# Layer 1 of a convolution and state-space kernel: transposes of delta x and sums of squares moved on TensorE, the first y sum of each group one step later, 432 instead of 416 tokens of the C products on VectorE

## The chip, the core and the metric

The kernel runs on one core of a Trainium2 chip. The core has TensorE (PE, matrix products and transposes), VectorE (DVE), ScalarE (ACT), GpSimd (POOL), SyncE (SP, which here issues the DMAs) and 16 DMA engines. The metric is the device time of one execution in microseconds; all data are float32.

## What is computed

Layer 0 is a block of convolutions on x of shape (32, 96, 56, 56). Layer 1, where the change lies, takes its result as 32 sequences of 3136 tokens with 96 channels and applies two blocks of this kind, then a 1x1 convolution with a batch normalisation:

```python
h = (seq - mu) * rsqrt(var + EPS) * ln_g + ln_b
xs, z = jnp.split(h @ in_w, 2, axis=-1)              # 192 channels each
xc = silu(sum(conv_w[:, k] * xp[:, k:k + L, :] for k in range(4)) + conv_b)
dbl = xc @ xproj_w                                   # dt, B (16), C (16)
delta = softplus(dt @ dt_w + dt_b)
dA = exp(delta[..., None] * A)
dBx = delta[..., None] * Bm[:, :, None, :] * xc[..., None]
hstates = associative_scan(comb, (dA, dBx), axis=1)[1]   # h = dA * h + dBx along the tokens
y = einsum('blds,bls->bld', hstates, Cm) + Dp * xc
seq = seq + (y * silu(z)) @ out_w
```

There are 192 x 16 = 3072 states per sequence, and each needs its own recurrence along the tokens.

## The kernel before

**Units and scans.** Each sequence is cut into four chunks of 784 tokens (`LC`). A unit is one chunk in one of the two blocks, so there are 256 units, in an order that alternates the blocks. In a unit the 3072 states are 24 tiles of 128 partitions (4 states by 32 channels). Each tile is one scan of 784 tokens on VectorE (L1052), one per step `at` of the main loop (L1134 on). `place` gives for step t of a unit a group k (of 64 channels, eight steps), j (which four states, two steps) and p (which 32 channels).

**Around one scan.** A scan needs da, an exponential of ScalarE (`decay`, L1004), and the input term. For j = 0 TensorE makes that term in PSUM (`fill`, L1018, 64 small matmuls of transposed u = delta x with diagonals of B). For j = 1 to 3 GpSimd makes it for two tiles at once (`inject`, bx, L1041). The states are then multiplied by C, two tiles at once: the first `LP` tokens on VectorE (`product`, L1060, with a copy cp of C that ScalarE puts into PSUM, `bring`, L1029), the rest on GpSimd (`rest`, L1068). TensorE sums the products over the states into y (`reduce`, L1099, 8 matmuls for two tiles). ScalarE starts each y with Dp x (`seed`, L1086), and VectorE multiplies the finished y by the gate (`gated`, L1110). There is one PSUM bank for y, so a seed waits for the gating of the group before. The fills are the scans 0, 1, 8, 9, 16 and 17 of a unit. A fill and a da tile of the other scans share two PSUM slots in turn, so fill t starts when scan t - 2 has ended.

**The order of the work** is written out by hand. In each step the loop issues, in this order: the steps of other units due below .05 of the step, the seed of tile at - 4 (`LAG` = 4), decays, the C copy, bursts, the scan, gating, VectorE's product, a save of the last state, GpSimd's product, the fill of the next step, the due steps from .05 to .08, the y sum of tile at - 4, and the other due steps. Each engine runs its own instructions in that order.

**The next unit is prepared meanwhile.** `prepare` gives each preparatory step a due time in steps; modulo 24 it tells at which scan of the running units it is issued. Those in question here: `center` (two matmuls per half, cen, L702) and `square` (ScalarE, sx, L707) at steps 12 to 14; `variance` (var, 14 matmuls with a single column, L712) at 14.06; `root` (L719 to 721) at 16.1, three small VectorE steps (`newton`) at 17.7; `turn_u` (ut, four transposes of u each, L848) at steps 19.5, 5.6 and 6.3 for the three groups, and `keep_u` (two ScalarE copies from PSUM, L854 and L855) half a step later. u itself is made by GpSimd (`input_u`, L864) at steps 9.5, 10.5 and 11.5. The results of such steps pass through two PSUM banks, taken in turn (`bank`). The convolution (xs, L773), the projections (bc L798, dt L810, z L789) and a burst of Silu or Softplus on ScalarE (L677, with table loads on either side) fall between. `finish` makes the output of a unit (o, L905 and L909) a unit later.

## Time and profile before

| | |
|---|---|
| median of 3 runs | 18177.14 us (18168.33 to 18189.24) |
| profiled execution, its own time | 18204.1 us |
| span in its trace | 18202.3 us |
| layer 1, first scan to end of the last | 3055.5 to 17903.5 us |
| granted TensorE clock, mean | 0.912 |
| busy VectorE, TensorE, ScalarE, GpSimd in 8000 to 12000 us | 3776.5, 3471.1, 3379.7, 3799.7 us |
| DMA engines' share, moved, in the same 4000 us | 0.71, 184 GB/s |
| mean C product on VectorE, on GpSimd | 998 ns, 1760 ns |
| mean C copy on ScalarE | 513 ns |

A line of a timeline has the start in us, the time taken, the engine, the line of the kernel, the operation, its tiles (out<-in) with their size, how many were merged, and in brackets the engine's idle time before it with what ended that. A line of the waits has the waiting engine and tile, what it waited for, the total in us, how often, and the longest. A line of the windows has the stretch, its length, the busy time of PE, PE's weight loads, DVE, ACT and POOL (with the number of instructions), then the granted TensorE clock, the DMA engines' share and GB/s.

### The profile page before, as it was taken

How to read it: one execution, taken by the hardware profiler on the slowest of the kernel's cores; microseconds unless marked ns; L12 is line 12 of the kernel's file. 1: busy time of each engine (PE TensorE's matmuls, PEld its weight loads, DVE VectorE, ACT ScalarE, POOL GpSimd, SP SyncE). 2: the span in 40 equal slices, each digit the busy share in tenths (PEclk: the TensorE clock that was granted, in tenths of full speed). 3: DMA queues.
4: the chain of work that ended last, by engine and by line, in shares of the span. 5: the costliest groups of instructions: out<-in, count | busy, mean ns of one | idle time of the engine just before them, and what ended most of it. 6: DMA issues, size and time to landing. Idle time of an engine off the chain costs nothing.

```text
span 18202.3 us, 515600 instructions
## 1 busy us (share of the span) xinstructions
PE 15733.6 (86%) x212542; PEld 8423.4 (46%) x212542; DVE 16751.8 (92%) x12755; ACT 14204.1 (78%) x26476; POOL 14151.6 (78%) x6254
## 2 busy tenths in 40 slices
PE   9999998888888888888888888888888888888882
PEld 4444444444444444444444444444444444444441
DVE  9999996999999999999999999999999999999993
ACT  5555555888888888888888888888888888888884
POOL 0000002999999999999999999999999999999993
PEclk9999998999999999999999999999999999999996
DMA  1111113777777777777777777777777777777768
GB/s 35 29 29 29 29 29 88 182 183 183 182 185 186 184 183 183 183 183 186 184 183 182 183 182 186 184 184 183 183 183 184 186 183 182 184 182 182 186 182 220
DMA packets 1723533, 2893.14 MB, mean 159 GB/s; under 512 B 712886, under 2 KB 950670, under 8 KB 1714790
## 3 DMA queue, kind: packets, MB, share of 16 engines
q1 hardware_dynamic: 1712534, 2821.54, 59.6%
q0 software_dynamic: 6656, 38.54, 1.0%
q8 instruction: 1668, 27.33, 0.6%
q14 instruction: 691, 5.66, 0.1%
q10 hardware_dynamic: 1984, 0.07, 0.0%
HBM read 2402.42 MB, written 455.82 MB: 157 GB/s over the span
## 4 chain that ended last, share of the span: by engine, by line
PE 22%; ACT 16%; issue 12%; DMA 11%; DVE 9%; SPq 7%; POOL 5%; ACTq 0%; POOLq 0%; DVEq 0%
PE bp L1018 9%; DVE hh L1052 5%; ACT da L1004 5%; ACT bx L1004 4%; SPq L982 4%; DVE hc L1060 3%; DMA bdiag<-bt 3%; DMA deltab<-deltad 3%; PE y L1099 3%; SPq L969 3%; POOL hc L1068 2%; POOL bx L1041 2%; PE bc L798 2%; PE o L909 2%; DMA C<-bcd 2%
## 5 line engine op out<-in xcount | busy, mean ns | idle before, releaser
L1041 POOL TENSOR_TENSOR bx<-ub,B 128x1568 f32<-128x1568 f32 x2304 | 8160.7, 3542 | 16.2 <-DMA B<-bcd 16.2
L1052 DVE TENSOR_TENSOR_SCAN hh<-da,state,bx 128x784 f32<-128x784 f32 x3456 | 6257.5, 1835 | 53.1 <-ACT da L1004 50.2
L1068 POOL TENSOR_TENSOR hc<-hh,C 128x736 f32<-128x736 f32 x3072 | 5407.9, 1760 | 747.9 <-DVE hh L1052 476.0
L1004 ACT ACTIVATE da<-deltab,acol 128x784 f32<-128x784 f32 x4608 | 4253.4, 923 | 1192.4 <-DVE hh L1052 1184.8
L1099 PE MATMUL y<-hc,rel 128*32 128x392 f32 x24576 | 2888.8, 544 | 551.0 <-ACT y L1086 547.4
L1018 PEld LDWEIGHTS bp<-diag,ut 91*32 91x32 f32 (+1 forms) x98304 | 2873.9, 131 | 931.9 <-DVE hh L1052 544.1
L1018 PE MATMUL bp<-diag,ut 91*32 91x91 f32 (+1 forms) x98304 | 3192.1, 293 | 116.6 <-DVE hh L1052 100.7
L1060 DVE TENSOR_TENSOR hc<-hh,cp 128x832 f32<-128x832 f32 x3072 | 3065.6, 998 | 0.1
L1052 DVE TENSOR_TENSOR_SCAN hh<-bx,state,bp 128x784 f32<-128x784 f32 x1152 | 2116.7, 1837 | 491.3 <-PE bp L1018 488.6
masks.py:197 POOL MEMSET eye<- 128x128 f32 x2 | 0.4, 204 | 2923.3 <-ACT x L427 2923.0
L773 PE MATMUL xs<-xn,wx 97*64 97x392 f32 x12288 | 2250.3, 508 | 0.5 <-ACT xc L784 0.4
L1052 DVE TENSOR_TENSOR_SCAN hh<-da,bx 128x784 f32<-128x784 f32 x1152 | 2017.9, 1774 | 29.6 <-ACT da L1004 28.1
L340 DVE SCALAR_TENSOR_TENSOR h<-hpad,hp,h 128x1568 f32<-128x1568 f32 x1024 | 1895.3, 1851 | 33.2
L1029 ACT COPY cp<-C 128x416 f32<-128x416 f32 x3072 | 1576.4, 513 | 95.6 <-DVE hc L1060 93.3
L1004 ACT ACTIVATE bx<-deltab,acol 128x784 f32<-128x784 f32 x1536 | 1467.8, 956 | 0.0
L773 PEld LDWEIGHTS xs<-xn,wx 97*64 97x64 f32 x12288 | 816.5, 137 | 1357.4 <-issue 1264.4
L1099 PEld LDWEIGHTS y<-hc,rel 128*32 128x32 f32 x24576 | 623.9, 118 | 1523.9 <-ACT y L1086 1044.7
L307 PE MATMUL dw<-hpad,diag 32*32 32x392 f32 x36864 | 1124.8, 525 | 0.6 <-issue 0.4
L1052 DVE TENSOR_TENSOR_SCAN hh<-bx,bp 128x784 f32<-128x784 f32 x384 | 683.0, 1779 | 244.2 <-PE bp L1018 228.3
L245 PE MATMUL c<-x,w 96*128 96x392 f32 x2048 | 785.3, 526 | 118.2 <-ACT hpad L252 96.2
L848 PE MATMUL ut<-eye,us 128*91 128x128 f32 (+1 forms) x3072 | 582.3, 320 | 340.7 <-ACT xc L784 340.3
L307 PEld LDWEIGHTS dw<-hpad,diag 32*32 32x32 f32 x36864 | 680.8, 106 | 375.4 <-issue 132.0
(195 smaller groups left out, 20083.7 us busy)
## 6 DMA issues: line engine op xcount, KB each, us to landing
ub<-ud SPq DMA_DIRECT2D x3072, 196.0 KB
deltab<-deltad SPq DMA_DIRECT2D x3072, 196.0 KB
C<-bcd SPq DMA_DIRECT2D x4096, 98.0 KB
diag<-bdiag SPq DMA_DIRECT2D x1024, 294.8 KB
B<-bcd SPq DMA_DIRECT2D x3072, 98.0 KB
deltad<-dl SPq DMA_DIRECT2D x512, 294.0 KB
ud<-us SPq DMA_DIRECT2D x1536, 98.0 KB
x<-in_x_dram SPq DMA_DIRECT2D x32, 1176.0 KB
```

The lines of the kernel that those rows point to most:

```text
L245: pe.matmul(ps[:p, k, :HB], w1[:, ct * 128 : ct * 128 + p], xs[b][:, c0 : c0 + HB], start=True, stop=True)
L307: pe.matmul(ps[r][to : to + 32, :HB], diag[src, n, t, :], hb[src, r0 : r0 + RB, dx : dx + W], start=t == 0, stop=t == 8, skip_group_check= ...
L340: v.scalar_tensor_tensor(acc, src, tap, acc, ALU.mult, ALU.add)
L773: pe.matmul(d["xs", k][h * 64 : h * 64 + 64, :HB], wx[:, i, o, k * 64 : k * 64 + 64], xn[:, o + h * HB : o + h * HB + HB], start=o == 0, s ...
L1004: s.activation(das[at], d["delta", k][:, p, :], AF.Exp, scale=acol[:, j, i, 2 * k + p : 2 * k + p + 1])
L1018: pe.matmul(ps[sg * DB : sg * DB + DB, o : o + z], d["ut", k][:z, b, h, p * DB : p * DB + DB], dg[:z, sg // 2, h, x : x + z, sg % 2], star ...
L1029: s.copy(cps[at], data[n]["C", j][:, :LP])
L1041: g.tensor_mul(bx, data[n]["u", k], beside(data[n]["B", j]))
L1052: v.tensor_tensor_scan(hhs[at - p][:, p, :], das.pop(at), bxs.pop(at), state[i][:, t : t + 1] if c % NQ else 0.0, ALU.mult, ALU.add,)
L1060: v.tensor_mul(hcs[at - 1][:, :, :LP], hhs[at - 1][:, :, :LP], beside(cps.pop(at)))
L1068: g.tensor_mul(hcs[at - 1][:, :, LP:], hhs[at - 1][:, :, LP:], beside(data[n]["C", j][:, LP:]))
L1099: pe.matmul(yps[k][r0 : r0 + DB, :HB], rel, hc[:, p, h * HB : h * HB + HB], start=False, stop=j == SG - 1, skip_group_check=True,)
```

## The change

Four edits, all in layer 1.

- `LP` goes from 416 to 432: VectorE multiplies 432 of 784 tokens by C, GpSimd 352, and the copy of C grows with it.
- The transposes of u (`turn_u`, `keep_u`) go to steps 13.06 and 14.06 (copies at 14.005 and 15.01) of the unit before for the first two groups, and to 19.5 (copy at 20.1) for the third.
- `variance` goes from step 14.06 to 15.06, which is after the fill of scan 16 and before the y sum in the same step; the second `center` goes behind the first transpose of its step.
- All seeds go one step later (`LAG` + 1), and so does the y sum of the tiles with j = 0; the other y sums stay.

```diff
-LP = 416
+LP = 432
...
-                steps += [((-11.9, -10.94)[h], lambda h=h: center(h)), ((-10.98, -9.99)[h], lambda h=h: square(h))]
-            steps += [(-9.94, variance), (-7.9, root), *[(t, lambda m=m: newton(m)) for m, t in enumerate((-6.3, -6.2, -6.1))]]
+                steps += [((-11.9, -10.93)[h], lambda h=h: center(h)), ((-10.98, -9.99)[h], lambda h=h: square(h))]
+            steps += [(-8.94, variance), (-7.9, root), *[(t, lambda m=m: newton(m)) for m, t in enumerate((-6.3, -6.2, -6.1))]]
...
-                steps += [((43.5, 53.6, 54.3)[k], lambda k=k: turn_u(k)), ((44.1, 54.2, 55.01)[k], lambda k=k: keep_u(k))]
+                steps += [((37.06, 38.06, 43.5)[k], lambda k=k: turn_u(k)), ((38.005, 39.01, 44.1)[k], lambda k=k: keep_u(k))]
...
-                if 0 <= at - LAG < total:
-                    seed(at - LAG)
+                if 0 <= at - LAG - 1 < total:
+                    seed(at - LAG - 1)
...
-                if 0 <= at - LAG < total:
-                    reduce(at - LAG)
+                for t in (at - LAG - 1, at - LAG):
+                    if 0 <= t < total and by_pe(t) == (t == at - LAG - 1):
+                        reduce(t)
```

## The prediction, as put on record

> **What bounds the kernel now.** I read the page's busy table first, then the sums of waits in a steady stretch (4,000 to 16,000 us), then the timelines of VectorE and TensorE through one unit, then the granted clock in the windows that stood out.

> ```profile
> PE 15733.6 (86%) x212542; PEld 8423.4 (46%) x212542; DVE 16751.8 (92%) x12755; ACT 14204.1 (78%) x26476; POOL 14151.6 (78%) x6254
> ```

> Layer 1 runs from 3,056 to 17,903 us: 256 units of 24 scans, 58.02 us each (mean of units 20 to 239; every "unit time" below is that mean, counted from the unit's scan 0). VectorE needs 24 scans, 12 C products, 3 gatings and 3 small steps. They fill 54.9 us; 3.16 us are waits. GpSimd is busy 54.9 us a unit too, so two engines have nearly the same bound. ScalarE and TensorE have room on average, not everywhere.

> ```profile
> DVE hh L1052 <- PE bp L1018: 586.0, 525, 2.3
> POOL hc L1068 <- DVE hh L1052: 383.1, 297, 2.9
> ```

> So VectorE waits mainly for a fill (bp), and GpSimd in turn for VectorE. By place, the mean waits are: scan 8 1.95 us, scan 16 0.59, scan 17 0.30 (fills), scans 18 and 20 0.31 (decays of ScalarE). TensorE just before scan 8, and VectorE beside it:

> ```profile
> 9041.66 0.86 PE L1099 MATMUL y<-hc,rel 128*32 128x392 f32 x8 [1.63 <-ACT y L1086]
> 9042.46 2.32 PE L773 MATMUL xs<-xn,wx 97*64 97x392 f32 x8
> 9044.71 1.11 PE L848 MATMUL ut<-eye,us 128*120 128x128 f32 x4
> 9046.33 1.11 PE L848 MATMUL ut<-eye,us 128*120 128x128 f32 x4 [0.52 <-ACT xc L784]
> 9047.37 2.76 PE L1018 MATMUL bp<-diag,ut 120*32 120x120 f32 x64
> 9049.96 0.83 PE L1099 MATMUL y<-hc,rel 128*32 128x392 f32 x8
> 9050.62 1.61 PE L1018 MATMUL bp<-diag,ut 120*32 120x120 f32 x64
> ```
> ```profile
> 9046.25 1.84 DVE L1052 TENSOR_TENSOR_SCAN hh<-da,state,bx 128x784 f32<-128x784 f32 x1
> 9050.28 1.85 DVE L1052 TENSOR_TENSOR_SCAN hh<-bx,state,bp 128x784 f32<-128x784 f32 x1 [2.19 <-PE bp L1018]
> ```

> Two things make this fill late. TensorE idles for the seed (y) and between the transposes (ut), so it starts late; and the same 64 matmuls take 2.76 us here, 1.61 a little later. The windows say why: first the idle one, then what followed, the same pair before scan 16, and a fill at full speed.

> ```profile
> 9039.66:9043.07 3.41, 1.78 (x16) 0.50 (x14) 3.41 (x4) 2.13 (x4) 3.41 (x2) 1.00 0.50 76
> 9043.07:9049.90 6.83, 6.32 (x78) 4.26 (x78) 5.02 (x4) 6.13 (x14) 6.06 (x4) 0.50 0.87 217
> 9063.55:9066.97 3.42, 2.10 (x57) 1.94 (x60) 3.42 (x4) 2.98 (x7) 3.42 (x4) 1.00 0.67 178
> 9066.97:9070.38 3.41, 3.41 (x72) 2.39 (x68) 3.41 (x3) 3.38 (x4) 3.41 (x2) 0.50 1.00 282
> 9030.02:9031.68 1.66, 1.66 (x68) 1.61 (x72) 1.66 (x2) 0.38 (x2) 1.66 (x2) 1.00 0.47 112
> ```

> The clock (PEclk, third number from the right) halves in steps of 3.41 us after a stretch with little streamed through the array. A fill then holds TensorE 2.57 us instead of 1.49 (start to next start), a y sum 1.3 instead of 0.8, the 14 matmuls of var 2.6 instead of 1.4.

> **The change, part by part** (unit times).

> *Transposes.* 12 transposes and 6 copies a unit move, none is added, no DMA with them. The four before scan 8, twice, leave that place (2.76 us with their waits), and ScalarE loses 1.5 us of copies there. *Seed and first sum a step on* (seed and 8 matmuls, three times a unit): ScalarE no longer stands 1.26 us at the seed for the gating; the decay of scan 6 starts at 10.55 when scan 4 ends, then decay of 8, cp, xc (0.92+0.93+0.51+0.48), and the seed ends at 13.8. TensorE: xs pieces end at 11.5, idle to 13.8, y to 14.6. The fill of scan 8 needs the slot that scan 6 leaves at 15.5. It starts then instead of at 17.1. Scan 8 is due at 18.15. At full clock the fill ends at 17.2, at half clock at 18.3. The 2.3 us idle before it will halve the clock often; by the windows above one busy window brings it back, so fill 9 (due 20.9) ends between 19.9 and 20.9. Wait at scan 8 and 9: 0 to 0.3, I take 0.1. Gain 1.85 us.

> *Variance behind the fill of 16, and two transposes in its place.* In step 14 the second transpose takes the bank that the first one holds (two banks in turn) and waits for its copy. That copy stands behind decay 14, decay 16 and cp on ScalarE: it ends at 32.0 (frame with scan 14 at 31.9). TensorE is idle from 30.0 to 32.0, transposes 0.6, then the moved y sum waits for its seed (33.0) and ends at 33.85. Then fill 16, var, y, fill 17 in one queue: 1.49+1.37+0.8+1.67 = 5.3 us at full clock, to 39.2. Scan 17 is due at 39.05: wait 0.1. Before, var had its waits ahead of fill 16. But 2.4 us idle out of 3.1 halves the clock for one window at nearly every phase; of 3.41 us about 2 to 3 fall on this queue and add 0.45 us each: 0.9 to 1.4. Bounds: 0.1 (full clock) and 3.2 (half clock for two windows). I take 1.35 for 16 and 17 together, nearest to the window pair shown, which has one halved window: 0.45 us worse than now.

> [...] The first window shown had 1.63 us idle in total and the next was at half clock, so I go by the row.

> *ScalarE behind it.* Two copies (0.75 each) join the stretch from 29 to 43 in which ScalarE is almost never idle, and a seed (0.6) only moves within it. The Silu burst (4.9 us) then starts at about 36.1 and decay 18 ends near 42.6, with scan 18 due at 42.7 after the late scan 17. The waits at 18 and 20 shrink from 0.31 to 0.1: gain 0.2. If fill 17 came early, this chain would be the next bound, at about 1.1 us of wait.

> *Third group.* Its first sum goes behind the dt matmuls, just ahead of fill 0. Fill 0 now ends about 0.8 us before scan 0 needs it; 0.8 of y eats that, but ScalarE frees dt 0.6 earlier. Cost 0 to 0.3; I take 0.

> *What the moved steps meet.* None of them issues a DMA, so SP's queue is passed by nothing. The transposes read products of GpSimd (L864), which end at 27.0 and 31.4 in the new frame, ahead of 28.5 and 32.0, when the banks are free. The later sums free an hc buffer about 2.4 us later; its next writer comes three products (some 14 us) on. The second centering matmul only goes behind a transpose of 0.6 us, in idle time. GpSimd's bx now ends 2.0 to 5.3 us before its scan; it doesn't move as far forward as VectorE does, and I find at least 1.0 left. All these: 0, and if that cover fails, at most the 0.3 us that stand in the range.

> *432 tokens.*

> ```profile
> L1068 POOL TENSOR_TENSOR hc<-hh,C 128x736 f32<-128x736 f32 x3072 | 5407.9, 1760 | 747.9 <-DVE hh L1052 476.0
> L1060 DVE TENSOR_TENSOR hc<-hh,cp 128x832 f32<-128x832 f32 x3072 | 3065.6, 998 | 0.1
> ```

> 32 of 832 elements more. From the gating's 392 in 534 ns to 832 in 998 the slope is 1.05 ns: +33 ns x 12 = 0.40 us a unit, all on the bound engine, 102 us in all. GpSimd's slope, from 736 in 1,760 to bx's 1,568 in 3,542, is 2.14 ns: -69 ns x 12 = -0.82 us, to 54.1. That covers GpSimd as next bound: its own waits for DMA are about 0.6 us a unit, and 54.7 is under the new period. The cp copy grows by some 18 ns x 12 on ScalarE, beside other work.

> *Sum.* -1.85 + 0.45 - 0.20 + 0.40 = -1.2 us a unit; x 256 = -307 us. The profiled execution took 18,204.1 us (span 18,202.3): 17,897. The median is 27 us lower: 17,870 us.

> **Rivals.**
> [...]
> 2. Nothing moves. 17 clock windows of 3.413 us are 58.03 us, and the unit lasts 58.02: waits and clock windows are locked to each other, since a unit that comes early meets the half clock at a worse place. If the new waits can still reach 2.8 us at some phase, the lock holds and the time stays 18,177, whatever was saved. For it: the phase of scan 0 to the windows stays within 0.6 us nearly all the way. Against: I find at most 2.3 us.
> 3. Slower. Fill 17 stands behind fill 16, var and y; if the clock is half for two windows there, it ends near 42.3 to 42.6 and the wait is 3.2 us instead of 0.9. That decides from 2.5 us upward (0.9 + 1.85 + 0.2 - 0.4). At 3.2 to 3.5: +0.6 to +1 us a unit, 18,330 to 18,430. For it: a slow window that is not well filled stays slow, and the y sum in front waits for its seed.

> **How the numbers follow.** Forecast 0.55 (scan 16 and 17 waits of 0.8 to 2.0 give 17,730 to 18,040), rival 1 0.13, rival 2 0.10, rival 3 0.22. About 0.2% is what a measurement can tell from no change. Faster 0.68, same 0.10, slower 0.22. The range takes all of the forecast and rival 2, rival 1 and the edge of rival 3: 17,550 to 18,260.

> **What would show it.** Right: no wait of scan 8 over 0.3 us in the mean; ut no longer between xs and bp ahead of scan 8; y sum at scan 5 gone and the wait of ScalarE for z (336 us) with it; waits of scan 17 of about a microsecond, with var between the fills; L1060 near 1,031 ns, L1068 near 1,690. Wrong: a unit of 58.03 us again (rival 2), or the largest wait now at scan 17 with TensorE at half clock (rival 3), or GpSimd's products waiting for nothing while VectorE waits for bx.

## The result, and the profile after

The changed kernel takes 18,437.06 us in the median of 4 runs (18,423.3 to 18,462.71), the kernel before 18,179.68 us beside it (18,168.33 to 18,189.24). The ratio is 1.0144 with an interval of 1.0131 to 1.0156: slower by 1.4%, where 17,870 us was forecast, and above the range of 17,550 to 18,260. It is the side of the third rival, a little above its 18,330 to 18,430.

The busy table of the kernel after, and its row for the core (span and mean granted TensorE clock; 0.912 before):

```profile
PE 15819.1 (86%) x212542; PEld 8541.3 (46%) x212542; DVE 16879.4 (92%) x12755; ACT 14224.5 (77%) x26476; POOL 13945.1 (76%) x6254
```
```profile
core 0: 18421.5 us, clock 0.900
```

The busy shares are those of before: TensorE shows 86% in both. What moved is the clock under it. The waits of the kernel after, in the same stretch of 4,000 to 16,000 us:

```profile
DVE hh L1052 <- PE bp L1018: 650.5, 686, 4.0
POOL hc L1068 <- DVE hh L1052: 409.9, 161, 3.4
```

VectorE still waits for fills, longer in all (586.0 before) and at worst 4.0 us instead of 2.3. By place, mean of units 20 to 239 of the profiled execution (as in all per-unit figures here; waits are those ahead of scans):

| us a unit | before | predicted | after |
|---|---|---|---|
| wait of scans 8 and 9 | 1.96 | 0.1 | 0.71 |
| wait of scans 16 and 17 | 0.89 | 1.35 | 2.37 (0.55 and 1.82) |
| wait of scans 18 and 20 | 0.31 | 0.1 | 0.28 |
| wait of scan 0 | 0 | 0 | 0.24 |
| VectorE's work, rest of the unit | 54.86 | +0.40 | 55.38 (+0.52) |
| unit | 58.03 | 56.8 | 58.98 |

Most of the wait at scan 8 went, and more came back at scan 17. It is uneven: 74 of the 220 units wait over 3 us there. TensorE in one of those, where scan 16 starts at 5,853.15 and scan 17 waits 3.95 us, to 5,859.89:

```profile
5848.67 0.63 PE L848 MATMUL ut<-eye,us 128*120 128x128 f32 x4 [1.90 <-POOL hc L1068]
5849.50 0.91 PE L1099 MATMUL y<-hc,rel 128*32 128x392 f32 x8 [0.20 <-ACT y L1086]
5850.19 2.85 PE L1018 MATMUL bp<-diag,ut 120*32 120x120 f32 x64
5852.96 2.78 PE L712 MATMUL var<-mean,sx 96*112 96x1 f32 x14
5855.67 1.53 PE L1099 MATMUL y<-hc,rel 128*32 128x392 f32 x8
5856.97 2.85 PE L1018 MATMUL bp<-diag,ut 120*32 120x120 f32 x64
```

The order is the predicted one (transposes, y, fill 16, var, y, fill 17), and so is the idle piece of 1.90 us ahead of it. From the fill of 16 on all takes its half-clock time. The windows of the same stretch (lengths, busy PE first, granted clock third from the right):

```profile
5846.79:5850.20 3.41, 1.32 (x15) 0.73 (x18) 3.41 (x3) 3.41 (x8) 3.41 (x3) 1.00 0.72 182
5850.20:5853.61 3.41, 3.41 (x72) 3.15 (x64) 2.88 (x3) 3.38 (x7) 3.41 (x2) 0.50 0.99 272
5853.61:5857.02 3.41, 3.41 (x24) 2.48 (x27) 2.33 (x2) 3.39 (x4) 3.41 (x3) 0.50 1.00 296
5857.02:5860.44 3.42, 3.42 (x76) 2.75 (x68) 0.55 (x1) 2.13 (x8) 2.00 (x1) 0.50 0.17 52
```

One window that is mostly idle is followed by three at half clock, and TensorE is occupied in all three from end to end. The second of them holds 24 instructions only: var, 14 records of one column each, takes most of it.

This is one of two kinds of unit. In the 74 units the queue, from the start of fill 16 to the end of fill 17, spends 9.5 us at half clock in the mean, and scans 16 and 17 wait 4.36 us together. In the other 146 it spends at most 3.1 us there, less than a window, and they wait 1.37 us. What parts the two is the phase: in each of the 74, fill 16 starts between 0.28 us ahead of a boundary between two clock windows and 0.16 us behind it, and in none of the 146.

Two rows of the products, GpSimd's and VectorE's:

```profile
L1068 POOL TENSOR_TENSOR hc<-hh,C 128x704 f32<-128x704 f32 x3072 | 5205.2, 1694 | 1204.9 <-DVE hh L1052 522.5
L1060 DVE TENSOR_TENSOR hc<-hh,cp 128x864 f32<-128x864 f32 x3072 | 3177.5, 1034 | 0.1
```

They are as predicted (1,031 and 1,690 ns). The 36 ns on VectorE, 12 times, are 0.43 us a unit; GpSimd's shorter product only adds to its idle time (1,204.9 us instead of 747.9).

### The profile page after: what moved, and what is told of

Same layout as the page of the kernel before. It is cut to its first block, busy times and chain, and to the rows that moved or that the text cites. A ratio compares the mean times of both kernels' runs of the same rounds, so it can differ in the third digit from the quotient of the medians.

```text
span 18421.5 us, 516623 instructions
## 1 busy us (share of the span) xinstructions
PE 15819.1 (86%) x212542; PEld 8541.3 (46%) x212542; DVE 16879.4 (92%) x12755; ACT 14224.5 (77%) x26476; POOL 13945.1 (76%) x6254
## 4 chain that ended last, share of the span: by engine, by line
PE 32%; issue 17%; DVE 15%; ACT 15%; DMA 3%; SPq 2%; POOL 2%; ACTq 0%; DVEq 0%; POOLq 0%
PE bp L1018 11%; DVE hh L1052 9%; PE y L1099 6%; DVE hc L1060 5%; ACT da L1004 3%; PE z L789 3%; PE bc L798 3%; PE o L909 3%; ACT bx L1004 2%; PE var L712 2%; PE o L905 2%; ACT sx_t L751 1%; PE dt L810 1%; ACT cp L1029 1%; PE cen L702 1%
## 5 line engine op out<-in xcount | busy, mean ns | idle before, releaser
L1052 DVE TENSOR_TENSOR_SCAN hh<-da,state,bx 128x784 f32<-128x784 f32 x3456 | 6270.8, 1838 | 44.8 <-ACT da L1004 43.0
L1068 POOL TENSOR_TENSOR hc<-hh,C 128x704 f32<-128x704 f32 x3072 | 5205.2, 1694 | 1204.9 <-DVE hh L1052 522.5
L1099 PE MATMUL y<-hc,rel 128*32 128x392 f32 x24576 | 3076.4, 576 | 695.4 <-ACT y L1086 542.6
L1018 PEld LDWEIGHTS bp<-diag,ut 91*32 91x32 f32 (+1 forms) x98304 | 3036.0, 135 | 1284.8 <-DVE hh L1052 773.5
L1018 PE MATMUL bp<-diag,ut 91*32 91x91 f32 (+1 forms) x98304 | 3276.3, 299 | 191.3 <-DVE hh L1052 190.2
L1060 DVE TENSOR_TENSOR hc<-hh,cp 128x864 f32<-128x864 f32 x3072 | 3177.5, 1034 | 0.1
L1052 DVE TENSOR_TENSOR_SCAN hh<-bx,state,bp 128x784 f32<-128x784 f32 x1152 | 2122.6, 1843 | 705.0 <-PE bp L1018 693.9
L773 PE MATMUL xs<-xn,wx 97*64 97x392 f32 x12288 | 2141.1, 497 | 0.5 <-ACT xc L784 0.5
L1052 DVE TENSOR_TENSOR_SCAN hh<-da,bx 128x784 f32<-128x784 f32 x1152 | 2019.2, 1777 | 24.7 <-ACT da L1004 23.1
L1029 ACT COPY cp<-C 128x432 f32<-128x432 f32 x3072 | 1619.1, 527 | 149.2 <-DVE hc L1060 136.3
L773 PEld LDWEIGHTS xs<-xn,wx 97*64 97x64 f32 x12288 | 835.2, 136 | 1283.3 <-issue 1192.6
L1099 PEld LDWEIGHTS y<-hc,rel 128*32 128x32 f32 x24576 | 606.9, 118 | 1596.7 <-ACT y L1086 1048.3
L848 PE MATMUL ut<-eye,us 128*91 128x128 f32 (+1 forms) x3072 | 511.4, 292 | 485.5 <-POOL hc L1068 316.3
L810 PE MATMUL dt<-bcs,wd 64*64 64x392 f32 x3072 | 684.6, 555 | 201.6 <-ACT xn L761 198.3
L864 POOL TENSOR_TENSOR us<-dl,xc 128x392 f32<-128x392 f32 x768 | 785.1, 1022 | 91.1 <-ACT dl L677 91.1
```

Source lines behind the costliest of these rows:

```text
L773: pe.matmul(d["xs", k][h * 64 : h * 64 + 64, :HB], wx[:, i, o, k * 64 : k * 64 + 64], xn[:, o + h * HB : o + h * HB + HB], start=o == 0, s ...
L810: pe.matmul(ps[r, :HB], wd[r, i, k, :], d["bcs"][r, :], start=True, stop=True)
L1018: pe.matmul(ps[sg * DB : sg * DB + DB, o : o + z], d["ut", k][:z, b, h, p * DB : p * DB + DB], dg[:z, sg // 2, h, x : x + z, sg % 2], star ...
L1029: s.copy(cps[at], data[n]["C", j][:, :LP])
L1052: v.tensor_tensor_scan(hhs[at - p][:, p, :], das.pop(at), bxs.pop(at), state[i][:, t : t + 1] if c % NQ else 0.0, ALU.mult, ALU.add,)
L1060: v.tensor_mul(hcs[at - 1][:, :, :LP], hhs[at - 1][:, :, :LP], beside(cps.pop(at)))
```

## The experiments

Two theories stood against each other. *The clock*: the change leaves idle pieces on TensorE ahead of the fills of 8 and 16, the clock halves there, and the fills behind come late. *The queue*: the order of work is at fault whatever the clock is, with the fill of 17 behind fill 16, var and y, and with late sums. All twelve in one table, with the per-unit figures (us) of the traces; a half window is a clock window of 3.413 us with a granted clock of 0.50 (in the traces of before and after the granted clock is 1.00 or 0.50 and changes only on a grid of 3.413 us). The kernel before, timed beside each of them, stood at 18,173 to 18,177 us.

| run | median us | ratio to before | unit | VectorE waits | half windows a unit |
|---|---|---|---|---|---|
| before | 18,180 | 1 | 58.03 | 3.16 | 2.89 |
| after | 18,437 | 1.0144 [1.0131, 1.0156] | 58.98 | 3.60 | 3.49 |
| e1_lp416 | 18,157.65 | 0.9986 [0.9974, 0.9998] | 57.69 | 2.68 | 2.78 |
| e2_var_back | 18,560.45 | 1.0211 [1.0196, 1.0226] | 59.49 | 4.07 | 4.02 |
| e3_warm | 17,697.92 | 0.9736 [0.9722, 0.9751] | 56.07 | 0.90 | 0.38 |
| e4_before_lp432 | 18,179.04 | 1.000 [0.9991, 1.0009] | 58.04 | 2.83 | 2.97 |
| e5_sums_back | 18,093.04 | 0.9955 [0.994, 0.997] | 57.68 | 2.39 | 2.07 |
| e6_transposes_only | 18,050.39 | 0.993 [0.9915, 0.9945] | 57.46 | 2.59 | 2.60 |
| e7_before_warm | 17,952.44 | 0.9874 [0.9858, 0.9891] | 57.13 | 2.04 | 1.29 |
| e8_warm_lp416 | 17,577.91 | 0.967 [0.9655, 0.9684] | 55.59 | 0.83 | 0.21 |
| e9_warm_b | 17,965.97 | 0.9886 [0.9871, 0.9901] | 57.17 | 1.66 | 2.03 |
| e10_warm_a | 18,041.33 | 0.9931 [0.9914, 0.9947] | 57.47 | 2.27 | 1.71 |
| e11_one_column | 18,485.42 | 1.017 [1.0154, 1.0185] | 59.19 | 3.81 | 3.62 |
| e12_warm_sums_back | 17,672.26 | 0.9725 [0.9711, 0.974] | 56.06 | 1.06 | 0.46 |

**The idle pieces filled.** The kernel after, with 14 matmuls a unit added whose results nobody reads (they write columns of a bank that hold no data), 6 behind the second `center`, 8 behind the last piece of xs. Each stands twice in the trace, like the other matmuls here (not the transposes), so the 6 are x12:

```diff
+        def warm(ps, times):
+            for _ in range(times):
+                pe.matmul(ps[:, HB:], eye, eye[:, : 512 - HB], start=True, stop=True, skip_group_check=True)
...
+                if h == 1:
+                    warm(ps, 6)
...
+                if k == NB - 1 and taps[-1] == KC - 1:
+                    warm(d["xs", k], 8)
```

> The changed kernel with idle TensorE time filled: 6 matmuls of 128x128 by 120 columns after the second centering matmul and 8 after the last xs piece, into unused columns of their banks, read by nobody. Clock theory: no half clock ahead of scans 8, 16 and 17; waits of 8 and 9 under 0.1 us together, 16 under 0.2, 17 under 0.9; unit 56.3 to 57.0 us, 17,750 to 17,930 us. Queue theory: TensorE gets more to do and the queue ahead of fill 17 stays as it is, scan 17 still waits 1.4 us or more: 18,430 to 18,600 us.

It took 17,697.92 us, 739 us less than the kernel after and 52 us under what the clock theory expected, with more work on TensorE and every other order the same. The core's row, VectorE's wait for fills, and TensorE through the same place as above (line numbers are shifted; L687 is the fillers):

```profile
core 0: 17707.0 us, clock 0.972
```
```profile
DVE hh L1060 <- PE bp L1026: 74.7, 147, 1.7
```
```profile
8914.36 1.50 PE L687 MATMUL cen<-eye 128*128 128x120 f32 x12
8916.46 0.62 PE L856 MATMUL ut<-eye,us 128*120 128x128 f32 x4 [0.60 <-POOL us L872]
8917.29 0.86 PE L1107 MATMUL y<-hc,rel 128*32 128x392 f32 x8 [0.20 <-ACT y L1094]
8918.44 1.65 PE L1026 MATMUL bp<-diag,ut 120*32 120x120 f32 x64 [0.29 <-DVE hh L1060]
8920.02 1.54 PE L718 MATMUL var<-mean,sx 96*112 96x1 f32 x14
8921.48 0.86 PE L1107 MATMUL y<-hc,rel 128*32 128x392 f32 x8
8922.16 1.66 PE L1026 MATMUL bp<-diag,ut 120*32 120x120 f32 x64
```

The queue fill 16, var, y, fill 17 stands unchanged and is now through in 5.4 us instead of 9.6 (5.5 instead of 7.2 in the mean); scan 17 waits 0.30 us. The queue alone is not the loss. The window with these fillers, and the next:

```profile
8913.66:8917.07 3.41, 2.81 (x20) 2.14 (x18) 3.41 (x4) 3.41 (x8) 3.41 (x3) 1.00 0.09 20
8917.07:8920.49 3.42, 2.93 (x78) 2.07 (x77) 3.42 (x3) 3.40 (x7) 3.42 (x4) 1.00 0.84 212
```

**The same fillers with one column.** A control for the 14 instructions as such: the same count and places, `ps[:, HB : HB + 1]` from `eye[:, :1]`.

> Control: the changed kernel with the same 14 filling matmuls a unit at the same places, but of one column instead of 120. Clock theory (what counts is what streams through the array): nothing streams, the clock halves as before, 18,437 plus or minus 80 us. Rival (more instructions on TensorE's queue help by themselves, as by keeping it from idling or changing its order): near 17,700 us.

18,485.42 us, near the kernel after and within the clock theory's 80 us of it. TensorE in a unit of it, the window with the fillers and the next, and the core's row:

```profile
9061.54 1.40 PE L687 MATMUL cen<-eye 128*128 128x1 f32 x12
9063.60 0.63 PE L856 MATMUL ut<-eye,us 128*120 128x128 f32 x4 [0.66 <-POOL hc L1076]
9064.42 1.53 PE L1107 MATMUL y<-hc,rel 128*32 128x392 f32 x8 [0.20 <-ACT y L1094]
9065.73 2.56 PE L1026 MATMUL bp<-diag,ut 120*32 120x120 f32 x64
```
```profile
9060.96:9064.37 3.41, 2.60 (x18) 2.02 (x18) 3.41 (x3) 3.41 (x9) 3.41 (x4) 1.00 0.33 75
9064.37:9067.79 3.42, 3.37 (x60) 2.43 (x64) 2.73 (x3) 3.40 (x7) 3.42 (x2) 0.50 0.94 241
```
```profile
core 0: 18495.5 us, clock 0.897
```

The fillers occupy TensorE for nearly as long (1.40 us against 1.50), the idle time that is left is nearly the same (0.66 against 0.60), and the window is busy 2.60 us against 2.81. Still the next one is at half clock, y takes 1.53 us and the fill 2.56. So here it is not the idle time as such that the half clock follows: what is streamed counts (0.50 behind fillers of one column, 1.00 behind fillers of 120).

**One place at a time.** Against e3, e9 keeps only the six fillers behind `center`, e10 only the eight behind xs:

```diff
                 if h == 1:
                     warm(ps, 6)
...
-                if k == NB - 1 and taps[-1] == KC - 1:
-                    warm(d["xs", k], 8)
```
```diff
-                if h == 1:
-                    warm(ps, 6)
...
                 if k == NB - 1 and taps[-1] == KC - 1:
                     warm(d["xs", k], 8)
```

> The changed kernel (432 tokens) with only the 6 filling matmuls after the second centering, ahead of scan 16. Clock theory with the loss in the queue of fill 16, var, y and fill 17: the waits of 16 and 17 fall from 2.4 us together to under 0.6, those of 8 and 9 stay at 0.7; 17,850 to 18,000 us. Rival (the half clock ahead of scan 8 is what carries the loss through the unit): 18,300 us or more.

> The changed kernel with only the 8 filling matmuls after the last xs piece, ahead of scan 8. Clock theory: the waits of 8 and 9 vanish (0.7 us), those of 16 and 17 stay near 2.4; 18,200 to 18,350 us. Rival (as for the other half): 17,800 us or less.

e9 gave 17,965.97 us: the waits of scans 16 and 17 fall to 0.29 together, no unit waits over 3 us at scan 17 any more, and 8 and 9 keep their 0.69. e10 gave 18,041.33 us, below what was expected: the waits of 8 and 9 vanish, and those of 16 and 17, expected to stay near 2.4, fall to 1.61, since scan 17 waits over 3 us in 50 units instead of 74. Why the fillers ahead of 8 help there was not tested; fill 16 starts 1.2 us earlier in the unit, so it can be the phase alone. Alone they gain 471 and 396 us, together 739: both places matter, the one ahead of 16 more.

**The parts of the change.** e1 takes LP back to 416 in the kernel after, e4 puts 432 into the kernel before:

```diff
-LP = 432
+LP = 416
```

> The changed kernel with 416 tokens of the C products again. Main theory (the lost time is the fill of scan 17, standing behind fill 16, var and a y sum at half clock): the C products take 0.42 us a unit less on VectorE, the waits stay, so 256 x 0.42 = 107 us come back: 18,330 us, still slower than before (18,180). Rival (the 16 tokens are most of the loss, since VectorE is the bound): 18,180 to 18,240. Third (units are locked to the clock windows): a saving on VectorE is eaten by longer waits, 18,400 to 18,440.

> The kernel before with 432 tokens alone. VectorE bound and waits fixed: 12 x 33 ns x 256 units = +102 us, 18,280 us. Locked to 17 clock windows of 3.413 us a unit: the waits shrink by what the products grow, 18,180 us plus or minus 20.

e4 costs nothing (1.000), as the locked theory said: VectorE has 0.35 us more work a unit and 0.33 less wait, and the unit stays at 58.04, which is 17 windows of 3.413 us. e1 gains 280 us on the kernel after, more than any of the three theories expected, where VectorE's work falls by 0.38 x 256 = 97 us; the waits fall by 0.92 us a unit and half windows from 3.49 to 2.78. Scan 17 waits over 3 us in 8 units instead of 74. The same 0.4 us of work is thus worth nothing in one kernel and 1.1 us a unit in the other (1.3 in the profiled execution of e1, 49 us under its median). The effects of the parts don't add up. That each part shifts the unit against the clock windows fits these counts, but no run varied the phase alone.

e2 puts the variance and `center` back ahead of the fill of 16, in the kernel after:

```diff
-                steps += [((-11.9, -10.93)[h], lambda h=h: center(h)), ((-10.98, -9.99)[h], lambda h=h: square(h))]
-            steps += [(-8.94, variance), (-7.9, root), *[(t, lambda m=m: newton(m)) for m, t in enumerate((-6.3, -6.2, -6.1))]]
+                steps += [((-11.9, -10.94)[h], lambda h=h: center(h)), ((-10.98, -9.99)[h], lambda h=h: square(h))]
+            steps += [(-9.94, variance), (-7.9, root), *[(t, lambda m=m: newton(m)) for m, t in enumerate((-6.3, -6.2, -6.1))]]
```

> The changed kernel with variance (and the second centering matmul) back in the places of before: var ahead of fill 16. Clock theory (var streams one column a matmul, so while it runs between the fills the half clock is kept up to three windows long): the wait of scan 17 falls from 1.8 us to 0.5 or less, scan 16 goes from 0.55 to 1.2 to 2.0; 18,260 to 18,350 us. Queue theory (var costs its length wherever it stands ahead of a fill): what leaves scan 17 comes back at scan 16, the sum of both stays at 2.1 to 2.6 us; 18,380 to 18,500 us.

18,560.45 us, above both: scan 17 waits 0.04 us now, but scan 16 waits 2.52. The sum of both, 2.55, is what the queue theory said (2.1 to 2.6), so at this clock var costs its time wherever it stands ahead of a fill; the clock theory's 1.2 to 2.0 for scan 16 was wrong. The move of the variance took 123 us off, with the rest of the change in place. The clock theory's number lay on the wrong side of the kernel after, and the rival's was passed at its upper end.

e5 puts seeds and sums back to the steps of before, in the kernel after:

```diff
-                if 0 <= at - LAG - 1 < total:
-                    seed(at - LAG - 1)
+                if 0 <= at - LAG < total:
+                    seed(at - LAG)
...
-                for t in (at - LAG - 1, at - LAG):
-                    if 0 <= t < total and by_pe(t) == (t == at - LAG - 1):
-                        reduce(t)
+                if 0 <= at - LAG < total:
+                    reduce(at - LAG)
```

> The changed kernel with the seeds and all y sums in the steps of before. Clock theory: the sum at scan 5 now splits the idle time ahead of fill 8 in two, but TensorE has no more to stream there, so the half clock ahead of scans 8 and 16 stays; scan 17 still waits over 1 us; 18,300 to 18,500 us. Rival (the late sums are what makes the fills late, since they stand in front of fills 8 and 16): the waits of 8, 9 and 16 vanish, 18,000 to 18,150 us.

18,093.04 us: 344 us less than the kernel after, within the rival's numbers and below the clock theory's. The waits of 8, 9 and 16 nearly vanish (0.21 together) and half windows fall from 3.49 to 2.07, but scan 17 still waits 1.85. Of the three edits undone singly (tokens, variance, sums), the late sums carried the most of the loss, and without them or without the 16 tokens the change is no longer slower than the kernel before. The longest idle piece in the 5 us ahead of fill 8 is 1.36 us in the mean without the late sums, 2.38 with them; ahead of fill 16 it is the same (1.86 and 1.87). e5 also takes the sums out from in front of the fills, as the rival says; e12 below puts that to the test.

e6 does only the moves of the transposes, in the kernel before:

```diff
-                steps += [((43.5, 53.6, 54.3)[k], lambda k=k: turn_u(k)), ((44.1, 54.2, 55.01)[k], lambda k=k: keep_u(k))]
+                steps += [((37.06, 38.06, 43.5)[k], lambda k=k: turn_u(k)), ((38.005, 39.01, 44.1)[k], lambda k=k: keep_u(k))]
```

> The kernel before with only the transposes moved (416 tokens, var and sums as before). If waits simply went with their cause, scan 8 would lose its 1.95 us and the rest stay: 256 x 1.9 = 490 us, 17,690 us. Clock theory: the two transposes leave TensorE idle ahead of fill 8 and bring new idle time (a wait for a bank) and var ahead of fill 16, so fills at half clock: scan 8 waits 0.3, scan 16 2 us or more; 18,250 to 18,500 us.

18,050.39 us, between the two expectations: scan 8 waits 0.06 us, and scan 16 waits 1.81 instead of 0.59. This line by itself makes the kernel before faster by 0.7%.

**Without the change, and the best of both.** e7 puts fillers of the same kind into the kernel before, again 14, ahead of the pieces that were late there:

```diff
+                if h == 1:
+                    warm(ps, 2)
...
+                    if k == 3:
+                        warm(ps, 5)
...
+                if k == 1 and taps[-1] == KC - 1:
+                    warm(d["xs", k], 7)
```

(The second pair stands in the loop of `variance`.)

> The kernel before, in its own order and with 416 tokens, with idle TensorE time filled: 7 matmuls of 128x128 by 120 columns ahead of the y sum at scan 5, 2 ahead of the one at scan 13, 5 in the wait within var, in unused columns of banks, read by nobody. Clock theory: no half clock, fills 1.67 us; scan 8 waits 0.6 to 0.9 (for the transposes alone), 16 and 17 under 0.3 together; unit 56.2 to 56.8, 17,720 to 17,870 us. Rival (order alone decides): scan 8 still waits 1.9 us, 18,150 us or more.

17,952.44 us, 80 us above the top of what was expected. Scan 8 came out as expected (0.68), but scans 18 and 20 wait 1.2 us for decays of ScalarE, and 1.29 half windows a unit are left, in places that these fillers don't reach. The places differ from those of e3, so the two don't compare the change with and without half clock cleanly.

e8 is e3 with the first edit below; e12 is e8 with the second, and with seeds and sums put back as in e5:

```diff
-LP = 432
+LP = 416
```
```diff
-                    warm(d["xs", k], 8)
+                    warm(d["xs", k], 5)
```

> The changed kernel with idle TensorE time filled, and with 416 tokens. If VectorE is the bound once the clock stays up, 0.40 us a unit come back against 432 tokens filled in the same way (17,698): 17,590 to 17,620 us. If GpSimd is (its products 69 ns longer, 54.9 us busy a unit plus waits for DMA): 17,690 to 17,750 us.

> The changed kernel with 416 tokens and filled idle time (5 matmuls in place of 8 after the last xs piece), and with seeds and sums in the steps of before. Clock theory: the step of the sums mattered through the idle time that it made, so with the clock up it is worth little: 17,578 plus or minus 60 us. Rival (a sum in front of a fill costs its 0.8 us at any clock): 17,350 to 17,450 us.

e8 took 17,577.91 us (17,562.6 to 17,584.1), a little below what was expected, 3.3% under the kernel before and the fastest here: VectorE works 54.76 us of a unit of 55.59. Against e3 it gains 120 us, 0.48 us a unit, of which the trace shows 0.41 in VectorE's work: with the clock up, the 432 tokens cost about what they weigh. e12 took 17,672.26 us, 94 us above e8, over the clock theory's 17,518 to 17,638 and far from the rival's 17,350 to 17,450. So with the clock up a sum in front of a fill does not lose, as it did without fillers. How much of the 94 us the three fillers fewer make (half windows 0.46 against 0.21) stays open.

## Why the prediction was wrong

**What failed, in its words:** "halves the clock for one window at nearly every phase; of 3.41 us about 2 to 3 fall on this queue and add 0.45 us each: 0.9 to 1.4 … I take 1.35". That holds in 146 of the 220 units: they have at most 3.1 us of half clock on the queue, and the two waits are 1.37 us, against the 1.35 taken. In the other 74 the half clock lasts three windows, as in the rows above, and the waits are 4.36 us. The step that failed is that the half clock ends after one window, whatever streams in it, in every unit. The same assumption stands in the part on scan 8, "by the windows above one busy window brings it back", though the first pair shown has 6.83 us, two windows, at 0.50, with TensorE busy 6.32 of them. In the trace of before, too, the queue from fill 16 to fill 17 spends more than a window at half clock in 132 of the 220 units (5.0 us in the mean).

The row that the prediction leaned on showed a halved window that was dense with matmuls of 91 to 392 columns; this queue has var in its middle, which occupies 2.78 us with 14 records of a single column. The mean of 2.37 us lies inside the bounds of 0.1 and 3.2, and nearer to the upper one, which the third rival stood for. It is 1.0 us a unit more than taken, 262 of the 567 us between 17,870 and 18,437. By itself this would have left a gain (18,132 us); the terms below made it a loss. e11 and e3 show what the clock went by here: with TensorE occupied for 2.60 us of a window by fillers of one column and other work the next is at 0.50, for 2.81 us with fillers of 120 columns at 1.00; what streams decided, and occupied time didn't. e3 has the predicted queue, 5.4 us against the 5.3 worked out, with 0.30 us of wait.

**Scans 8 and 9**: moving the transposes and the seed gave the times that were said. ScalarE's wait for the gating (336 us) is gone, the seed ends at 13.9 us of the unit (13.8 predicted), the fill of 8 starts at 15.59 (15.5). But it takes 2.78 us: the idle 2.3 us that the prediction saw halved the clock, and 0.71 us are left instead of 0.1. That is 0.61 x 256 = 156 us. In e10 the same order at full clock has no wait there. The late sum, counted as a help here, is what left the 0.71: with the sums in their old steps and the transposes moved, scans 8 and 9 wait 0.08 us in e5 and 0.07 in e6.

**Third group**, "Cost 0 to 0.3; I take 0": 0.24 us at scan 0, 61 us. The late sum makes it (0.01 us in e5, with the sums back), and half clock doesn't: fill 0 takes 1.66 us in the mean, and e3 waits 0.28 us there.

**The transposes' bank.** "It ends at 32.0": the second transpose waited for its bank in all 220 units, as predicted, and started 99 to 100 ns after the first one's copy ended (98 to 117 at most), though the profile names GpSimd as what ended the wait in 177 of them, and nothing in 43. The copy ended at 33.1 in the unit's mean, not at 32.0, with scan 14 at 32.7 instead of 31.9, and the idle piece was close to what was predicted (1.9 us, for 2.0).

**ScalarE behind it**: 0.28 us at scans 18 and 20 instead of 0.1; another 46 us. **432 tokens**: 0.43 us for the products, 0.52 with the other VectorE work, for 0.40: 31 us, and no other engine was next. In sum 262 + 156 + 61 + 46 + 31 = 556 of 567 us. These are differences between waits of one trace and the forecast; as the experiments show, they would not come back one by one.

**The rivals.** The third was right on sign and place, scan 17, and in a third of the units on the clock: "a slow window that is not well filled stays slow" (the window of 24 instructions at 0.50, and the next at 0.50 too). Its number was partly luck. It took two half windows and a wait of 3.2 to 3.5 us in all units, and by its own sum no mean wait under 2.5 us makes the change slower; the mean was 2.37, and the loss came about because the other terms fell short as well. It got 0.22 because the estimate was put on the one pair with a single halved window. The second was right about the kernel before, as e4 bears out, and wrong about the change: after it the unit no longer holds to 58.03 us, but moves between about 56.5, 58 and 61.5 us in a pattern of some 16 units. The first, with 0.13, was a clock that stays up: by the author's estimate from the waits in the trace of before 1.55 to 2.4 us less a unit, 17,560 to 17,780 us. It was wrong in the kernel after (0.900), and e3 is the kernel in which it nearly holds (0.972): 17,698 us.

**The row followed.** The prediction went by a row in which 1.63 us of idle time had the half clock behind them. The trace after shows the same: 1.32 of 3.41 us busy, in gaps of at most 1.90 us, and the next windows at 0.50. The row held in direction and not in length.

Whether the slow windows would also go by replacing var's single columns with something dense was not tried.

## What to carry over

Before moving work off TensorE or behind another engine, look at the windows of granted clock around the place: the price of an idle piece is paid by what stands behind it, at 1.7 to 1.8 times its time here (a fill 2.85 us instead of 1.66, a y sum 1.53 instead of 0.86), until a window comes that streams enough; fillers of one column did not make such a window in e11 (18,485 us), fillers of 120 did in e3 (17,698). When a queue holds matmuls of one column, as var here, cost it both with one window at half clock and with the whole queue at half clock, and ask at which phases each holds: here two thirds of the units were of the first kind and a third of the second. Try a few unread wide matmuls in the idle piece ahead of it. Where a loop runs against the clock windows like this, don't add up single edits: about 0.4 us of work showed nothing in one kernel and nearly three times its weight in the other.
